# A four-layer graph network on one core: the check of the adjacency lists, with a count on VectorE replaced by a sum on ScalarE

## The chip, the cores and the metric

The kernel runs on one core of a Trainium2 chip. The metric is the device time of one execution in microseconds (us). The engines are named as in the profile: PE is TensorE (PEld its weight loads), DVE is VectorE, ACT is ScalarE, POOL is GpSimd, SP is SyncE, which here issues most DMAs. A `q` behind an engine's name (SPq, ACTq) is its sequencer, which issues DMAs and waits on semaphores.

## The reference, cut to what matters

The input `x` has 16 batches of 1024 nodes by 256 features, and `adj` is one 1024 x 1024 float32 matrix that all batches share. An entry of `adj` is either zero or lies between 0.05 and 0.19; a row has 16.7 entries on average, 30 at most, and none is negative. Layer 0 is the one that the change belongs to:

```python
pre_u = jnp.einsum('bud,dk->buk', h_t, W1[:d])
pre_v = jnp.einsum('bvd,dk->bvk', h_t, W1[d:])
hidden = jax.nn.relu(pre_u[:, :, None, :] + pre_v[:, None, :, :] + b1)
S = jax.nn.sigmoid(jnp.einsum('buvk,ko->buvo', hidden, W2)[..., 0] + b2[0])
a_t = jnp.einsum('buv,bud->bvd', S * A_a, h_t)          # A_a is adj
m_t = jnp.einsum('uv,bud->bvd', A_m, h_t) * h_t          # A_m is adj
z_t = beta1 * h_t + beta2 * (a_t @ Wa + ba) + beta3 * (m_t @ Wm + bm)
```

Since `S` is multiplied by `adj`, the scores of an edge matter only where `adj` isn't zero. Layer 1 multiplies by `adj` and a weight, with a relu and a residual; layers 2 and 3 are graph attention with a softmax over `leaky_relu(f_i + f_j) + adj`.

## The kernel before, in words

Everything is float32. A stage of preparation comes first; after it a branch (`tc.If(listed > 0)`, L688) chooses between a path by lists, which computes the edge scores only at the non-zero entries, and a dense path that computes all of them. With these inputs the lists are taken.

The preparation (L375 to L516) has two threads that are interleaved in the source.

The first thread is layer 0's projections of the first group of four batches (`first_group`, L381). For each batch, PE transposes `h` (16 transposes, L310), ACT copies the four banks into `hT` (`evacuate`, L143; in this stage `by_scalar` is true, so all four copies are ACT's), and `edge_sides` (L315) multiplies `hT` by `w1`: 64 matmuls (L131) per batch, whose banks ACT copies into `st` (L333, L334), and whose results SP stores to DRAM. `hT` is the stationary operand of these matmuls, so none can begin before its copy is done.

The second thread makes the lists: for each of the eight 128-row tiles of `adj` (`adj_sb[:, t, :]`, loaded by SP at L392 behind the first two batches of `x`), DVE finds the 32 largest entries of each row by four MAX8 (L451) and three MATCH_REPLACE8 (L453). At L447 it also counts the row's non-zero entries, into `there`. Afterwards (L473 to L503) a few small DVE instructions and three small matmuls (L468, L470, L489) work out whether the lists hold everything: the number of positive slots must equal the number of entries, no value may occur twice in a row, none may exceed 16, and the rows with more than 16 entries must fit a table. The result is `ok`, which every engine loads (L518) before the branch.

The generator `work` is stepped by `more(n)` at fixed places in the source, but the order in which the instructions stand on each engine is not the source's: the framework schedules the whole program statically, engine by engine, by estimated ready times. An engine then takes its instructions strictly in that order, each waiting on the semaphores that it names.

After the branch, PE's work is ordered by hand (messages, edges, layer 1, attention), and the edge scores (gathers by POOL, adds by DVE, sums by ACT) are paced beside it by a `Side` object that spends a fixed share of a step per microsecond of PE's estimated work. Many of the loads are tied to matmuls by `paced`.

Of the kernel before, what the change touches and what calls it, by code (L numbers as in the profile page):

```python
# [11 lines left out]
F32 = mybir.dt.float32  # L12
I32 = mybir.dt.int32
U32 = mybir.dt.uint32
AF = mybir.ActivationFunctionType
ALU = mybir.AluOpType
AX = mybir.AxisListType
P = 128
# [6 lines left out]
SLOTS = 32  # L25
# [45 lines left out]
def gnn_stack_kernel(  # L71
# [27 lines left out]
    nc = tc.nc  # L99
    B, N, D = x.shape  # L100
    NT = N // P
# [174 lines left out]
    slot_a = const.tile([P, NT, SLOTS], F32, name="slot_a")  # L276
# [98 lines left out]
    with ExitStack() as stack:  # L375
        prep = stack.enter_context(tc.tile_pool(name="prep", bufs=4))
        prep1 = stack.enter_context(tc.tile_pool(name="prep1", bufs=1))
# [54 lines left out]
        def clear():  # L432

            if zeros:
                paced(nc.scalar.dma_start(zeros.pop(0), zero))

        def more(n):
            for _ in range(n):
                next(work, None)


        there = prep1.tile([P, NT], F32, name="there")
        for t in range(NT):
            more(4)
            row = adj_sb[:, t, :]
            left = prep.tile([P, N], F32, tag="left", name="left")
            nc.vector.tensor_scalar(left, row, 0.0, 0.0, ALU.not_equal, ALU.add, accum_out=there[:, t : t + 1])  # L447
            src = row
            for r in range(SLOTS // 8):
                s = slice(8 * r, 8 * r + 8)  # L450
                nc.vector.max(out=slot_a[:, t, s], in_=src)  # L451
                if r < SLOTS // 8 - 1:
                    nc.vector.match_replace(  # L453
                        out=left, in_to_replace=slot_a[:, t, s], in_values=src, imm_value=-1.0
                    )
                    src = left
            if t > 2:
                clear()
                clear()
# [13 lines left out]
        held = prep1.tile([P, NT, SLOTS], F32, name="held")  # L473
        nc.vector.tensor_scalar(held, slot_a, 0.0, None, ALU.is_gt)
        counts = prep1.tile([P, 4], F32, name="counts")
        nc.vector.tensor_reduce(counts[:, 0:1], held, AX.XY, ALU.add)
        nc.vector.tensor_reduce(counts[:, 1:2], there, AX.X, ALU.add)
        nc.vector.tensor_reduce(counts[:, 2:3], slot_a[:, :, 0], AX.X, ALU.max)
        twice = prep1.tile([P, NT, SLOTS - 1], F32, name="twice")
        nc.vector.tensor_tensor(twice, slot_a[:, :, 1:], slot_a[:, :, : SLOTS - 1], ALU.is_equal)  # L480
        nc.vector.tensor_tensor(twice, twice, held[:, :, 1:], ALU.mult)
        nc.vector.tensor_reduce(counts[:, 3:4], twice, AX.XY, ALU.add)
        missed = prep1.tile([P, 1], F32, name="missed")
        nc.vector.tensor_tensor(missed, counts[:, 0:1], counts[:, 1:2], ALU.not_equal)
        nc.vector.tensor_tensor(missed, missed, counts[:, 3:4], ALU.add)
        nc.vector.scalar_tensor_tensor(missed, counts[:, 2:3], TOP, missed, ALU.is_gt, ALU.add)
        more(1)
# [951 lines left out]
    with arm.Else():  # L1439
        with ExitStack() as stack:  # L1440
            wide = stack.enter_context(tc.tile_pool(name="dwide", bufs=9))
            row = stack.enter_context(tc.tile_pool(name="drow", bufs=6))
# [124 lines left out]
```

## Time and profile before

| what | value |
|---|---|
| median of 3 runs | 3131.87 us (3128.81 to 3140.97) |
| the profiled execution, its own time | 3123.77 us |
| its span in the trace | 3122.0 us |
| granted TensorE clock in it | 0.998 |
| busy: PE, PEld, DVE, ACT, POOL | 3071.5, 2181.0, 2422.3, 1821.7, 1894.7 us |
| preparation: last matmul of the first group ends, branch taken | about 101.6 us from the span's start |

The profile's times are those of one execution. A row of the timeline gives the start and the duration in us, the engine, the source line, the operation, the tiles written and read, how many instructions the row merges, and in brackets how long the engine had been idle before it and what released it. A row of the windows gives for one stretch the busy time of each engine, the granted clock, and the busy share and the rate of the DMA engines.

### The profile page before, as it was taken

The page shows a single profiled execution, that of the slowest core. Times are in us where ns is not written, and L with a number is a line of the kernel's source. Part 1 is how long each engine was busy: PE and PEld are TensorE (multiplying, and loading weights), DVE is VectorE, ACT ScalarE, POOL GpSimd, SP SyncE. Part 2 cuts the span into 40 slices and gives each one's busy share as a digit, 9 for nine tenths or more (in the row PEclk, how much of TensorE's full clock was granted, in tenths as well). Part 3 has the DMA queues.
Part 4 walks back from the last instruction along what each step waited for, and adds up shares of the span by engine and source line. Part 5 has one row for each costly group of instructions (what it writes and reads, how often), then busy time and mean ns, then how long its engine had stood idle before and what let it go on. Part 6 is the DMA issues. An engine that isn't in the chain of part 4 may idle for free. (4 is left out here: it accounts for less than half of the span.)

```text
span 3122.0 us, 39040 instructions
## 1 busy us (share of the span) xinstructions
PE 3071.5 (98%) x11954; PEld 2181.0 (70%) x11954; DVE 2422.3 (78%) x3247; ACT 1821.7 (58%) x6456; POOL 1894.7 (61%) x1483
## 2 busy tenths in 40 slices
PE   8999999999999999999999999999999999999999
PEld 5544545545547756888875688887568888858888
DVE  7887777778776878999887899988789983257844
ACT  3345555566655766777667677766667762214242
POOL 1156778777665777667677776676777751076600
PEclk9999999999999999999999999999999999999999
DMA  9998888888889777558977655897765554475500
GB/s 322 330 339 302 278 296 266 272 248 254 263 268 347 233 224 209 155 163 279 304 234 214 201 160 166 271 301 236 215 196 157 165 205 158 137 254 158 162 1 28
DMA packets 288420, 699.96 MB, mean 224 GB/s; under 512 B 46141, under 2 KB 141178, under 8 KB 281034
## 3 DMA queue, kind: packets, MB, share of 16 engines
q0 software_dynamic: 128224, 387.80, 42.0%
q1 hardware_dynamic: 132538, 258.46, 23.5%
q10 hardware_dynamic: 27440, 51.13, 4.4%
q8 instruction: 96, 1.57, 0.2%
q14 instruction: 122, 1.00, 0.1%
HBM read 565.83 MB, written 131.41 MB: 223 GB/s over the span
## 5 line engine op out<-in xcount | busy, mean ns | idle before, releaser
L831 ACT ACTIVATE z<-z 128x256 f32<-128x256 f32 x2432 | 979.7, 406 | 585.6 <-DVE z L827 523.0
L825 DVE TENSOR_TENSOR z<-z,u 128x1024 f32<-128x1024 f32 x608 | 738.3, 1219 | 299.1 <-PE bank L131 174.4
L131 PE MATMUL bank<-feats,m 128*128 128x257 f32 x4096 | 908.7, 380 | 1.1 <-ACT feats L1016 0.7
L708 POOL DMA_INDIRECT z<-v_d,slot_v x512 | 665.4, 1300 | 367.1 <-ACT z L831 196.8
L131 PEld LDWEIGHTS bank<-feats,m 128*128 128x128 f32 x4096 | 769.5, 190 | 111.1 <-ACT feats L1016 1.5
L713 POOL DMA_INDIRECT dense_d<-gt,slot_at x512 | 682.5, 1333 | 196.4 <-issue 139.3
L827 DVE SCALAR_TENSOR_TENSOR z<-z,w2r 128x1024 f32<-128x1024 f32 x608 | 737.3, 1219 | 9.3
L131 PE MATMUL bank<-gc,hw 128*128 128x256 f32 x2048 | 451.1, 382 | 14.9 <-ACT gc L1133 10.2
L831 ACT ACTIVATION_READ_ACCUMULATOR z<-z 128x1 f32 x2432 | 461.6, 190 | 0.0
L131 PE MATMUL bank<-adj_sb,h 128*128 128x512 f32 x1024 | 443.0, 592 | 4.4 <-ACT st L333 2.1
L131 PEld LDWEIGHTS bank<-gc,hw 128*128 128x128 f32 x2048 | 388.8, 191 | 76.8 <-ACT gc L1133 13.3
L1099 DVE SCALAR_TENSOR_TENSOR m<-rho,tau,adj_sb 128x512 f32<-128x512 f32 x512 | 375.7, 742 | 66.0 <-PE bank L131 61.7
L131 PE MATMUL bank<-adjT_in,y 128*128 128x512 f32 (+1 forms) x960 | 402.0, 579 | 5.3 <-DMA adjT_in<-adjT_d 3.6
L131 PEld LDWEIGHTS bank<-adj_sb,h 128*128 128x128 f32 x1024 | 194.1, 190 | 244.8 <-issue 239.0
L131 PEld LDWEIGHTS bank<-adjT_in,y 128*128 128x128 f32 x960 | 181.5, 190 | 219.4 <-issue 206.4
L131 PE MATMUL bank<-w,hT 128*128 128x512 f32 (+1 forms) x1024 | 334.0, 486 | 0.0
L131 PEld LDWEIGHTS bank<-w,hT 128*128 128x128 f32 x1024 | 194.5, 190 | 140.9 <-issue 121.9
L1133 ACT ACTIVATE gc<-gd 128x1024 f32<-128x1024 f32 x64 | 133.2, 2082 | 169.9 <-PE bank L131 104.2
L131 PE MATMUL bank<-g_wT,z 128*128 128x257 f32 x1024 | 230.1, 380 | 0.0
L131 PEld LDWEIGHTS bank<-g_wT,z 128*128 128x128 f32 x1024 | 192.2, 190 | 30.0 <-issue 2.9
L708 POOL DMA_INDIRECT z<-v_d,x_node x96 | 125.0, 1303 | 116.8 <-ACT z L831 61.0
L1131 DVE COPY gc<-gd 128x1024 f32<-128x1024 f32 x64 | 71.8, 1122 | 105.8 <-PE bank L131 79.3
(169 smaller groups left out, 2439.1 us busy)
## 6 DMA issues: line engine op xcount, KB each, us to landing
gd<-dense_d SPq DMA_DIRECT2D x128, 512.0 KB
dense_d<-zero ACTq DMA_DIRECT2D x64, 512.0 KB
adjT_in<-adjT_d SPq DMA_DIRECT2D x112, 256.0 KB
h<-in_x_dram SPq DMA_DIRECT2D x19, 1024.0 KB
u_d<-st SPq DMA_DIRECT2D x64, 256.0 KB
v_d<-st SPq DMA_DIRECT2D x64, 256.0 KB
hw_d<-st SPq DMA_DIRECT2D x64, 256.0 KB
u<-u_d POOLq DMA_DIRECT2D x32, 512.0 KB
```

What stands on the lines that cost most here:

```text
L131: recent.append(nc.tensor.matmul(*args, **kw))
L708: return nc.gpsimd.indirect_dma_start(out=dst, out_offset=None, in_=src[:], in_offset=bass.IndirectOffsetOnAxis(ap=at, axis=0), **how,)
L713: return nc.gpsimd.indirect_dma_start(out=dst[:], out_offset=bass.IndirectOffsetOnAxis(ap=at, axis=0), in_=src, in_offset=None,)
L825: paced(nc.vector.tensor_tensor(z, z, u, ALU.add))
L827: nc.vector.scalar_tensor_tensor(zk, zk, 0.0, w2r[:, None, :].to_broadcast([P, GB, D]), ALU.max, ALU.mult)
L831: nc.scalar.activation(zk[:, c, :], zk[:, c, :], AF.Copy, accum_out=s[:, k, c : c + 1])
L1099: nc.vector.scalar_tensor_tensor(m, r[:, cols], ta[:, kt : kt + 1], ea[:, kt, cols], ALU.max, ALU.mult)
L1131: paced(nc.vector.tensor_copy(gc, by_batch), 16)
L1133: paced(nc.scalar.activation(gc, by_batch, AF.Copy), 16)
```

## The change

The count of non-zero entries on DVE (L447) goes. In its place ACT computes relu(-adj) of each tile of rows and accumulates it along the row into `below_zero`; the elements themselves go to a scratch tile `gone` that nothing reads. The test behind it is another one: instead of comparing two counts, it asks whether any row's 32nd largest entry, or any row's sum of negative parts, is above zero. (A row of exactly 32 entries passes the old test and fails the new one; the densest row of these inputs has 30.)

```diff
-        there = prep1.tile([P, NT], F32, name="there")
+        below_zero = prep1.tile([P, NT], F32, name="below_zero")
+        gone = prep1.tile([P, N], F32, name="gone")
         for t in range(NT):
             more(4)
             row = adj_sb[:, t, :]
             left = prep.tile([P, N], F32, tag="left", name="left")
-            nc.vector.tensor_scalar(left, row, 0.0, 0.0, ALU.not_equal, ALU.add, accum_out=there[:, t : t + 1])
+            nc.scalar.activation(gone, row, AF.Relu, scale=-1.0, accum_out=below_zero[:, t : t + 1])
...
-        nc.vector.tensor_reduce(counts[:, 0:1], held, AX.XY, ALU.add)
-        nc.vector.tensor_reduce(counts[:, 1:2], there, AX.X, ALU.add)
+        nc.vector.tensor_reduce(counts[:, 0:1], slot_a[:, :, SLOTS - 1], AX.X, ALU.max)
+        nc.vector.tensor_reduce(counts[:, 1:2], below_zero, AX.X, ALU.max)
...
-        nc.vector.tensor_tensor(missed, counts[:, 0:1], counts[:, 1:2], ALU.not_equal)
+        nc.vector.tensor_tensor(missed, counts[:, 0:1], counts[:, 1:2], ALU.max)
+        nc.vector.tensor_scalar(missed, missed, 0.0, None, ALU.is_gt)
```

In the built program the eight new activations stand first on ACT, ahead of the copies of the first batch's `hT`. The start of ACT's order, before and after (`x8`: eight in a row):

```text
before                                   after
L160 DMA w1 (three issues)               L160 DMA w1 (three issues)
table load                               table load
L143 hT<-bank x4                         L447 gone,below_zero<-adj_sb x8
L333 st<-bank, L334 st<-bank, ...        L143 hT<-bank x4
                                         L333 st<-bank, L334 st<-bank, ...
```

Each of the eight waits for the load of its own tile of rows, and from the second on also for the one before it, since all write `gone`. The orders on PE, POOL and SP are unchanged, and DVE's is the old one without L447, but for a few of the small instructions of the test. One wait of SP moves: the load of the second batch's `h` behind the branch (L290) now waits for the preparation's last use of memory that its `hT` (L299) waited for before.

## The prediction

> **What bounds the kernel now.** I read the page first, for the bound of the whole. Then I took the timelines of PE, ACT and DVE over the first 102 us, where the change lies, and the windows of the stretch in which `adj` arrives.
>
> ```profile
> PE 3071.5 (98%) x11954; PEld 2181.0 (70%) x11954; DVE 2422.3 (78%) x3247; ACT 1821.7 (58%) x6456; POOL 1894.7 (61%) x1483
> ```
>
> PE is busy for 98% of the span, so a stage is worth what it does to PE. The PE timeline of the preparation:
>
> ```profile
> 10.91 1.54 PE L310 MATMUL bank<-ident,h 128*128 128x128 f32 x6 [1.69 <-DMA h<-in_x_dram]
> 12.24 21.50 PE L131 MATMUL bank<-w,hT 128*128 128x512 f32 x64
> 33.58 1.91 PE L310 MATMUL bank<-ident,h 128*128 128x128 f32 x16
> 35.33 20.81 PE L131 MATMUL bank<-w,hT 128*128 128x512 f32 x64
> ...
> 98.75 2.83 PE L131 MATMUL bank<-w,hT 128*128 128x512 f32 x8
> 102.06 7.21 PE L228 MATMUL bank<-ident,adj_sb 128*128 128x128 f32 x64 [0.47 <-ACT st L334]
> ```
>
> The products of batch 0 start at 12.24, and from there PE runs without a gap until 101.6: four batches of 64 matmuls and 16 transposes, then the first work behind the branch at 102.06. PE sets the length of the preparation. The products wait for copies by ACT, whose timeline has two of batch 0's at the top and those of batch 1, four in a row, below:
>
> ```profile
> 7.96 0.60 ACT L143 ACTIVATE hT<-bank 128x512 f32<-128x512 f32 x1 [4.29 <-PE bank L310]
> 8.82 0.60 ACT L143 ACTIVATE hT<-bank 128x512 f32<-128x512 f32 x1 [0.26 <-PE bank L310]
> ...
> 34.22 2.06 ACT L143 ACTIVATE hT<-bank 128x512 f32<-128x512 f32 x4
> ```
>
> So the first two copies, all that the first products need, are done by 9.4. DVE, which makes the lists beside this:
>
> ```profile
> 18.63 1.22 DVE L447 TENSOR_SCALAR_CACHE_REDUCE left<-adj_sb 128x1024 f32<-128x1024 f32 x1 [8.53 <-DMA adj_sb<-in_adj_dram]
> 21.00 1.22 DVE L447 TENSOR_SCALAR_CACHE_REDUCE left<-adj_sb 128x1024 f32<-128x1024 f32 x1
> ...
> 96.15 0.19 DVE L491 COPY total<-bank 128x32 f32<-128x32 f32 x1 [0.98 <-PE bank L470]
> ```
>
> DVE can't begin before the first tile of `adj` lands at 18.63, is then busy without a break until 95.2, and waits 0.98 us for PE's L470 before the last part of the test. It is nearly as long as PE's thread, but it is PE that comes last. The windows say when the rest of `adj` can be there (the last number is the DMA rate in GB/s):
>
> ```profile
> 18.00:20.00 2.00, 2.00 (x7) 1.02 (x6) 1.37 (x3) 0.42 (x2) 0.75 (x2) 1.00 0.92 323
> 20.00:22.00 2.00, 2.00 (x8) 1.18 (x8) 2.00 (x2) 0.98 (x2) 0.00 (x0) 1.00 1.01 364
> 22.00:24.00 2.00, 2.00 (x8) 1.30 (x7) 2.00 (x5) 0.98 (x2) 0.00 (x0) 1.00 1.01 367
> 24.00:26.00 2.00, 2.00 (x8) 1.30 (x7) 2.00 (x4) 0.60 (x1) 0.00 (x0) 1.00 1.02 404
> 26.00:28.00 2.00, 2.00 (x8) 0.99 (x7) 2.00 (x4) 0.62 (x2) 0.00 (x0) 1.00 1.06 375
> 28.00:30.00 2.00, 2.00 (x7) 1.13 (x6) 2.00 (x3) 0.74 (x2) 0.00 (x0) 1.00 1.09 349
> ```
>
> Behind the first tile, seven of 512 KB are to come, 3.67 MB. Filled at these rates from 18.63 on, they are in at 28.6 if nothing else is moved. If the 1 MB of batch 2's `x`, which SP issues at 18.63, comes in between, it is 2.9 us more, 31.5. The trace's record of semaphore updates has the last of the sixteen updates of the last tile at 29.2, and I take that.
>
> **What the change adds: a wait at the head of ACT.** In the built order the eight activations stand ahead of batch 0's four copies. ACT takes its instructions in order, so the copies now wait for the last tile of `adj`, though they need nothing of it. Step by step:
> 1. The last tile lands at 29.2. The tiles come 1.51 us apart on average ((29.2 - 18.63) / 7).
> 2. One activation with its sum costs 1.045 + 0.187 = 1.23 us, by these two rows (ns, least, median, most), the first of the same shape, the second of the read of the accumulator. That is less than 1.51, so the earlier seven are done when the last tile comes, and the eighth ends at 30.45.
>
> ```profile
> L870 ACT ACTIVATE u<-b1r x56: 1039/1045/1084, 102.4 to 2422.0; 128x1024 f32<-128x1024 f32 x56
> L831 ACT ACTIVATION_READ_ACCUMULATOR z<-z x2432: 183/187/252, 148.0 to 2560.5; 128x1 f32 x188
> ```
>
> 3. Two copies from banks that have long been full: 0.60 for one and 2.06 for four gives 0.49 per further one, so 1.09, and 31.55.
> 4. PE loads `hT` as weights, 0.19, and multiplies from 31.75 on, where it was 12.24: **19.5 us later**. With the bounds of the landing it is 18.9 to 21.8.
>
> Queued behind ACT's wait are PE's products of all four batches, the stores of `hT`, `st` and the zeros, the three small matmuls of the test (between the last products), and so `ok` and the branch, for which every engine waits. PE has no gap from 12.24 to 101.6 in which to catch up, so all of that comes 19.5 us later. The loads of `adj` and of batches 2 and 3 stand ahead of these stores on SP's queue and don't move.
>
> The restart itself: the windows show a granted clock of 1.00 throughout, the idle start included, and batch 0's products took 21.50 against 20.81 for batch 1's, so at most 0.69 us is paid for the start today. Today's start also comes out of idle time (1.69 us just before, and more ahead of it), so I add nothing for the new one. A rule speaks against that: the Trainium skill, "TensorE: Matmul & The Clock Gate", section "What's actually happening", has an array that was idle for some 3.4 us at half clock until it has been busy for about as long. By it a restart after 19 us of idleness loses 1.7 us, an estimate from that page, and the shift would be 20.5.
>
> **What it removes from DVE.** Eight L447, 1.15 us each from start to start (18.63 to 19.78), are 9.2 us. In the test a sum over 256 columns of 0.41 becomes one over 8 (0.15 by its neighbour L477), and one instruction of 0.15 is added: 0.1 less together. DVE's thread then ends at 85.9 instead of 95.2. But its next instruction waits for L470, which moves from 95.73 to 115.2, so the time saved becomes idle time, and I credit nothing. If PE weren't the bound of the preparation, up to 9.3 us would be gained.
>
> The moved wait of SP (batch 1's `h`) is for the preparation's last products, done before SP gets there; `gone` is 4 KB per partition, and the orders show nothing else that it displaces. Both at nothing; should the wait decide once, it is in the upper end.
>
> **The sum.** The profiled execution's own time, 3123.77, becomes 3143.3. The median of the runs is 8.1 above it, and I carry the shift over: 3131.87 + 19.5 = **3151.4 us**, 0.62% more. About 0.5%, 15.7 us, is what a measurement of this kernel can tell from no change.
>
> **The rivals.**
> *Given back behind the branch (not slower).* From 102 to 150 PE is busy for only 41.5 of 48 us and the DMA engines are full (share 1.02); it is the one place where PE waits for transfers. If the later start let these drain ahead, PE could win back at most the 6.5 us that it idles there: 13.0 left, 3144.9, within 0.5%. It decides from 3.8 us won back. Against it: everything that fills the DMA engines there is issued behind the branch or paced by matmuls, and the rate is 0 GB/s from 100 to 102, so there is no backlog that more time could drain. 12 in 100.
>
> *The activations don't keep up.* ACT also has a row of 128x1024 at 2.08 us (L1133, strided). At 2.08 + 0.19 the eight need 18.2 us from 18.63, and end at 36.8 instead of 30.45: 6.3 more, 25.8 in all, 3157.7. Against it: `adj_sb` and `gone` are read and written in a row, as L870's are. 6 in 100.
>
> *The gain on DVE counts and the wait doesn't.* If ACT had all of `adj` before its first copy, at about 8 us, and DVE were the bound, 9.3 us fewer: 3122.6, within 0.5%. The first tile lands at 18.63, so the row itself speaks against it. 2 in 100.
>
> *The change doesn't do what it says.* A row of 32 entries would fail the new test and send the kernel down the dense path: 16 x 1024 x 2 relus of 128x1024 at about 1.1 us on two engines are 18 ms. The densest row has 30. Under 1 in 100.
>
> **How the numbers follow.** The forecast has 79 in 100. Of that some 3 fall under 15.7 by the scatter of the runs (12 us between three of before). Some of the larger rivals are over 0.5% as well, so slower gets 0.81; the first and third rival and those 3 give 0.17 for no change; 0.02 is left for faster by something that I don't see. The range runs from 3143 (the first rival, 3144.9, less 2 of scatter) to 3161 (the second, 3157.7, with 3 of scatter); the bounds of the landing, 3150.8 to 3153.7, lie inside.
>
> **What would show it.** In the changed profile ACT should have eight activations of `gone` (L448 in the changed file) between about 18.7 and 30.5, at 1.05 and 0.19 us, before its first L143; PE's first products should start near 31.7, the transposes being done at 12.4; DVE should wait near 29 us for PE's second small matmul; the first transposes of `adj` should start near 121.6 (102.06 + 19.5); and any later landmark, such as the first sum of layer 1 or the end, should be late by the same. It would be wrong if PE's products start before 25, if the delay shrinks between 120 and 170, or if the activations end long after the last tile.

## The result, and the profile after

The changed kernel takes 3161.77 us (median of 7 runs, 3150.25 to 3164.08), the kernel before beside it 3139.5 (7 runs, 3128.81 to 3147.49). The ratio is **1.0067, 95% interval [1.0051, 1.0083]**: slower by 16 to 26 us, where 19.5 were forecast. The time itself lies 10.4 us over the forecast of 3151.4. Of that, 7.6 are the kernel before, which ran at 3139.5 here and not at the 3131.87 that the forecast started from; the difference between the two kernels, which the forecast is about, is 22.3 between the medians. In the second set of experiments below the ratio was 1.0055 [1.0041, 1.0070].

PE's timeline of the changed kernel, cut as that of before (start, duration, what, idle time before it and its releaser):

```profile
10.73 1.54 PE L310 MATMUL bank<-ident,h 128*128 128x128 f32 x6 [1.27 <-DMA h<-in_x_dram]
30.38 22.93 PE L131 MATMUL bank<-w,hT 128*128 128x512 f32 x64 [18.11 <-ACT hT L143]
53.15 1.91 PE L310 MATMUL bank<-ident,h 128*128 128x128 f32 x16
54.90 20.81 PE L131 MATMUL bank<-w,hT 128*128 128x512 f32 x64
...
118.32 2.83 PE L131 MATMUL bank<-w,hT 128*128 128x512 f32 x8
121.62 7.20 PE L228 MATMUL bank<-ident,adj_sb 128*128 128x128 f32 x64 [0.47 <-ACT st L334]
```

The transposes are done at 12.3 as before. Then PE stands still for 18.11 us, for a copy by ACT. From batch 1 on the rows are those of before, 19.57 us later (54.90 against 35.33), and so are the first transposes behind the branch, 19.56 (121.62 against 102.06). What ACT does meanwhile, the first and the last of the eight activations:

```profile
18.75 1.06 ACT L448 ACTIVATE gone<-adj_sb 128x1024 f32<-128x1024 f32 x1 [15.08 <-DMA adj_sb<-in_adj_dram]
19.72 0.19 ACT L448 ACTIVATION_READ_ACCUMULATOR gone<-adj_sb 128x1 f32 x1
...
28.70 1.06 ACT L448 ACTIVATE gone<-adj_sb 128x1024 f32<-128x1024 f32 x1
29.66 0.19 ACT L448 ACTIVATION_READ_ACCUMULATOR gone<-adj_sb 128x1 f32 x1
29.75 2.04 ACT L143 ACTIVATE hT<-bank 128x512 f32<-128x512 f32 x4
```

ACT idles 15.08 us for the first tile of `adj`, while the banks that it could copy fill up, all four by 12.3. The copies start at 29.75. And DVE, which was to be relieved:

```profile
85.92 0.16 DVE L488 SCALAR_TENSOR_TENSOR missed<-counts,missed 128x1 f32<-128x1 f32 x1
115.72 0.19 DVE L493 COPY total<-bank 128x32 f32<-128x32 f32 x1 [29.65 <-PE bank L471]
```

It is through with its lists at 86.1 instead of 95.2, and waits 29.65 us for PE instead of 0.98.

This one profiled execution has a span of 3162.4 us, 40.4 more than the one of before, and only half of that stands at the branch. The sums of edge scores on ACT, matched one by one between the two traces, are 19.4 us late at 148 us, 25.4 at 723, 31.0 at 908, 28.8 at 1124 and 39.4 at the end. I take what is added behind the branch for scatter of this execution and not for a part of the change: the medians differ by 22.3 us, and the profile of the same kernel in the second set (e6_after) has a span of 3146.6, 24.6 more than that of before. The last section says what the scatter goes with.

### The profile page after: what moved, and what is told of

It reads as the page before. It is cut to its first block, busy times and chain, and to the rows that moved or that the text cites. A ratio compares the mean times of both kernels' runs of the same rounds, so it can differ in the third digit from the quotient of the medians.

```text
span 3162.4 us, 39048 instructions
## 1 busy us (share of the span) xinstructions
PE 3083.4 (98%) x11954; PEld 2186.0 (69%) x11954; DVE 2414.5 (76%) x3232; ACT 1831.1 (58%) x6472; POOL 1905.9 (60%) x1483
## 3 DMA queue, kind: packets, MB, share of 16 engines
q8 instruction: 96, 1.57, 0.2%
## 5 line engine op out<-in xcount | busy, mean ns | idle before, releaser
L710 POOL DMA_INDIRECT z<-v_d,slot_v x512 | 653.7, 1277 | 370.6 <-ACT z L833 202.2
L131 PEld LDWEIGHTS bank<-gc,hw 128*128 128x128 f32 x2048 | 390.1, 192 | 83.0 <-ACT gc L1135 12.3
```

The lines of the kernel that those rows point to most:

```text
L131: recent.append(nc.tensor.matmul(*args, **kw))
L710: return nc.gpsimd.indirect_dma_start(out=dst, out_offset=None, in_=src[:], in_offset=bass.IndirectOffsetOnAxis(ap=at, axis=0), **how,)
```

## The experiments

My theory: the loss is a wait, for the last tile of `adj`, at the head of ACT's queue; it delays PE's first products, and the delay is carried unchanged to the end. The rivals: the work of the eight activations, the scratch tile or the new test costs it wherever they stand; the saving on DVE is a gain that the wait hides; the idle start brings on a slower clock later. The first four kernels ran on one chip, the last two on another, each set with the kernel before beside it.

**e1_late: the same work, without the wait at the head.**

```diff
-            nc.scalar.activation(gone, row, AF.Relu, scale=-1.0, accum_out=below_zero[:, t : t + 1])
+            paced(nc.scalar.activation(gone, row, AF.Relu, scale=-1.0, accum_out=below_zero[:, t : t + 1]))
```

`paced` adds a wait for a recent product. In the built order the first activation then stands behind the copies of batch 0's `hT`, and the other seven are spread over the four batches.

> The changed kernel with its eight activations tied to matmuls of the first group, so that in the built order they stand between the copies of the four batches and no longer ahead of batch 0's. Nothing else differs; the same work is done. Theory (the loss is the wait at the head of ScalarE's queue): PE's first products start near 12.2 us again, the first transposes of adj near 102, and the time is that of the kernel before within 0.2%. Rival (the eight activations, the new test or the scratch tile cost this wherever they stand): still 0.5 to 0.8% slower, about 20 us.

Measured: 3134.82 us (12 runs) against 3128.13 (29), ratio 1.0021 [1.0005, 1.0037]. PE's first products and the first transposes of `adj`:

```profile
12.55 22.14 PE L131 MATMUL bank<-w,hT 128*128 128x512 f32 x64
...
103.15 7.21 PE L228 MATMUL bank<-ident,adj_sb 128*128 128x128 f32 x64 [0.47 <-ACT st L334]
```

The 20 us at the branch are gone but for 1.1 (0.3 in the start, 0.6 in batch 0's products). The time, though, lay 4.8 us over before by the means and 6.7 by the medians, with an interval clear of zero, which the theory hadn't in it. The mean granted clock of its runs was lower, 0.9960 against 0.9967. So the kernel was run again.

**e5_late_again: the same kernel once more.**

> The kernel of e1_late once more, to settle whether its 0.21% [0.05, 0.37] over before is real. Theory (only the wait costs; the branch was 1.1 us late in e1_late, from the phase of the slow clock at the start): 0 to 0.1%, with an interval that holds zero or nearly so. Rival (the eight activations, the scratch tile or the new test cost some 5 us behind the branch wherever they stand): again 0.15 to 0.25%, and the changed kernel beside it would owe the same 5 us to them, so that its branch comes 16 and not 19.6 us late.

Measured: 3132.17 us (12 runs) against 3132.16 (17), ratio 1.0003 [0.9991, 1.0015].

```profile
11.75 22.35 PE L131 MATMUL bank<-w,hT 128*128 128x512 f32 x64
...
102.56 7.21 PE L228 MATMUL bank<-ident,adj_sb 128*128 128x128 f32 x64 [0.47 <-ACT st L334]
```

The surplus of e1_late did not come back, and this time the clocks were alike (0.9967 against 0.9965). When they don't stand in front of PE's first copies, the eight activations, the scratch tile and the new test cost little: the two sets together, weighted by their intervals, give some 0.1% and at most 0.2% (an estimate: 3 us, at most 6), and not 20 us. Whether it is nothing or 3 us stays open.

**e2_wait: the wait, without the work.** The kernel before, with two lines more:

```diff
         there = prep1.tile([P, NT], F32, name="there")
+        seen = prep1.tile([P, 1], F32, name="seen")
+        nc.scalar.activation(seen, adj_sb[:, NT - 1, 0:1], AF.Copy)
```

> The kernel before, count on VectorE and old test included, with one 128x1 copy of an element of the last tile of adj put first on ScalarE: the wait alone, with some 0.2 us of work. Theory: ScalarE is held until the last tile lands at 28.7 us; with 0.2 for the copy and 0.6 for the first eviction PE starts near 29.6 instead of 12.2, batch 0's products take 22.9 instead of 21.5 as in the changed kernel, and everything behind is 18 to 19 us late: 0.5 to 0.7% slower. Rival (the work, not the wait): no more than 0.2 us, so the same as before.

Measured: 3149.88 us (6 runs) against 3128.13, ratio 1.0065 [1.0042, 1.0088]. ACT's timeline and PE's:

```profile
28.82 0.20 ACT L444 ACTIVATE seen<-adj_sb 128x1 f32<-128x1 f32 x1 [25.14 <-DMA adj_sb<-in_adj_dram]
28.93 2.04 ACT L143 ACTIVATE hT<-bank 128x512 f32<-128x512 f32 x4
```

```profile
29.56 23.97 PE L131 MATMUL bank<-w,hT 128*128 128x512 f32 x64 [16.91 <-ACT hT L143]
...
121.84 7.21 PE L228 MATMUL bank<-ident,adj_sb 128*128 128x128 f32 x64 [0.47 <-ACT st L334]
```

One instruction of 0.20 us costs as much as the whole change: 21.75 between the medians against 22.3. PE starts at 29.56, where 29.6 was expected, and the branch is 19.78 us late. This is the plainest evidence for the theory and against the work.

**e3_one: the activation for the first tile alone.** The sums of the other seven tiles are left out.

```diff
-            nc.scalar.activation(gone, row, AF.Relu, scale=-1.0, accum_out=below_zero[:, t : t + 1])
+            if t < 1:
+                nc.scalar.activation(gone, row, AF.Relu, scale=-1.0, accum_out=below_zero[:, t : t + 1])
...
-        nc.vector.tensor_reduce(counts[:, 1:2], below_zero, AX.X, ALU.max)
+        nc.vector.tensor_reduce(counts[:, 1:2], below_zero[:, 0:1], AX.X, ALU.max)
```

> The changed kernel with the activation for the first tile of adj alone; the sums of the other seven tiles are left out, and the test looks at the one sum. Theory (what counts is which tile is waited for): the first tile lands at 18.7 us, 1.25 for the activation and 0.6 for the first copy give PE's first products near 20.6, 8.4 later than before, and with a slow restart of up to 1.4 the branch is 8.4 to 9.8 late: 0.25 to 0.35% slower. Rival (the work): an eighth of 20, 2.5 us.

Measured: 3138.63 us (12 runs) against 3128.13, ratio 1.0029 [1.0014, 1.0045], which is 4.4 to 14 us.

```profile
20.73 22.45 PE L131 MATMUL bank<-w,hT 128*128 128x512 f32 x64 [8.06 <-ACT hT L143]
...
111.49 7.21 PE L228 MATMUL bank<-ident,adj_sb 128*128 128x128 f32 x64 [0.47 <-ACT st L334]
```

With the first tile to wait for, the branch is 9.43 us late, and the time 9.1 us more by the ratio (0.0029 x 3128.13). The rival's 2.5 lies outside the interval. What is waited for sets the cost. Of the work, only the last activation stands in the path, between the landing and the copies: the copies of the changed kernel start 1.05 us behind the start of its eighth activation (28.70 to 29.75).

**e4_no_count: the saving on DVE alone.** The kernel before, with the count and the comparison left out and nothing put in their place but the test of the 32nd largest:

```diff
-            nc.vector.tensor_scalar(left, row, 0.0, 0.0, ALU.not_equal, ALU.add, accum_out=there[:, t : t + 1])
...
-        nc.vector.tensor_reduce(counts[:, 0:1], held, AX.XY, ALU.add)
-        nc.vector.tensor_reduce(counts[:, 1:2], there, AX.X, ALU.add)
+        nc.vector.tensor_reduce(counts[:, 0:1], slot_a[:, :, SLOTS - 1], AX.X, ALU.max)
...
-        nc.vector.tensor_tensor(missed, counts[:, 0:1], counts[:, 1:2], ALU.not_equal)
+        nc.vector.tensor_scalar(missed, counts[:, 0:1], 0.0, None, ALU.is_gt)
```

> The kernel before without the count and with nothing in its place: the sum on VectorE and the comparison with it are left out, and the test asks only whether a 32nd largest entry is above zero. Theory (VectorE's 9.2 us are off the path, since its next instruction waits for a matmul between PE's last products): VectorE waits some 10 us instead of 1 for that matmul, the first transposes of adj start at 102 as before, and the time is the same within 0.2%. Rival (the saving on VectorE is a gain that the wait hid in the changed kernel): 9 us faster, 0.3%.

Measured: 3132.46 us (12 runs) against 3128.13, ratio 1.0005 [0.9990, 1.0020]. DVE's timeline, and PE's behind it:

```profile
96.31 0.19 DVE L488 COPY total<-bank 128x32 f32<-128x32 f32 x1 [10.34 <-PE bank L468]
```

```profile
102.22 7.21 PE L228 MATMUL bank<-ident,adj_sb 128*128 128x128 f32 x64 [0.47 <-ACT st L334]
```

The 9.2 us have turned into idle time (10.34 instead of 0.98), the branch stands where it stood, and a gain of 9 us (0.3%) is outside the interval. There was nothing for the change to win on DVE.

**e6_after: the changed kernel on the chip of e5_late_again.**

> The changed kernel itself, on the same chip as e5_late_again. Theory: the first transposes of adj 19 to 21 us later than 102, the median 19 to 22 us over before, and 17 to 21 us over e5_late_again. Rival (half of the 40 us between the two profiles is a slower clock that the idle start brings on later in the run): the mean granted clock of its runs is lower than before's by 0.002 or more, and the difference nearer 30 us.

Measured: 3149.81 us (6 runs) against 3132.16 (17), 17.65 more; ratio 1.0055 [1.0041, 1.0070]; 17.64 over e5_late_again.

```profile
30.49 23.21 PE L131 MATMUL bank<-w,hT 128*128 128x512 f32 x64 [18.27 <-ACT hT L143]
...
122.01 7.21 PE L228 MATMUL bank<-ident,adj_sb 128*128 128x128 f32 x64 [0.47 <-ACT st L334]
```

The branch is 19.95 us late; the difference of the medians is 1.4 us under the expected range, and the interval (12.8 to 21.9 us) holds 19.95. The mean granted clock of its six runs is 0.9963, that of the 17 of before 0.9965, and e2_wait, which has the same idle start, had 0.9968 against 0.9967. So the idle start doesn't bring on a slower clock later, and that rival falls. (The seven runs of the changed kernel in the result had 0.9954; for the kernel before beside them the clocks aren't on record, so that set can't say.)

No version came out that beats both kernels; the best of the changed ones, e5_late_again, equals the kernel before within its interval.

## Why the prediction was right, point by point

*The path.* Right. The landmarks that show it stood where the prediction had them, or near: the activations between 18.75 and 29.85 (18.7 and 30.5), the first transposes of `adj` at 121.62 (121.6), DVE's wait 29.65 (29). Two did not. PE's first products came at 30.38 and not near 31.7, for the reasons below, and the end of the profiled execution was 40.4 us late and not 19.5. Of the wait, the runs show that it alone is enough (e2_wait) and that without it little or nothing is lost (e5_late_again).

*The terms of the sum.* The total at the branch was right to 0.1 us, partly by luck, since three terms were off and cancelled.
- The landing of the last tile was taken as 29.2, from the record of semaphore updates in the profile of before. By the same record it was 28.61 in the changed kernel and 28.80 in e2_wait, so it moves by some tenths of a us from run to run. The windows alone had given 28.6.
- Step 3 counted two copies before the first product. PE's products begin behind the first: the copies start at 29.75, PE at 30.38. Each product takes one half of the features, and the first of a pair needs only the first copy, 0.49 us less. With copies that start 0.70 earlier (29.75 against 30.45), and a weight load of 0.19 that the start of PE's row turned out to include (the rows of the first product and of its weight load both start at 30.38), this put PE's start 1.37 us too late (31.75 against 30.38).
- "I add nothing" for the restart was wrong, by 1.43 us: batch 0's products took 22.93 us, not 21.50.

*The clock of the restart.* The reason for that last miss is worth a look. PE's weight loads of these products (start, duration):

```profile
33.11 0.34 PEld L131 LDWEIGHTS bank<-w,hT 128*128 128x128 f32 x1 [0.52 <-DVE slot_a L452]
...
35.52 0.19 PEld L131 LDWEIGHTS bank<-w,hT 128*128 128x128 f32 x1 [0.24 <-issue]
```

and the windows of the same stretch, whose granted clock is the third number from the end:

```profile
30.00:34.00 4.00, 3.62 (x5) 1.55 (x6) 4.00 (x6) 1.79 (x4) 0.00 (x0) 1.00 1.00 355
```

The first loads take 0.34 instead of 0.19, and from start to start they are 0.85 us apart (33.11 to 33.96) instead of 0.43 (35.52 to 35.95). So the array runs at half speed there, while the window says 1.00. The trace's list of clock records explains it: the first one, at full clock, begins at 34.50 (13.63 in the profile of before), and where there is no record the window shows 1.00. I had read that default as a measurement. With the start of the first record, the cost of the restart follows in all eight profiles: it is half the time from PE's first product to that record (all in us).

| profile | first product | first full-clock record | half the time between | batch 0's products less 20.81 |
|---|---|---|---|---|
| before | 12.24 | 13.63 | 0.70 | 0.69 |
| e4_no_count | 11.84 | 14.37 | 1.26 | 1.25 |
| e1_late | 12.55 | 15.24 | 1.35 | 1.33 |
| e5_late_again | 11.75 | 14.86 | 1.56 | 1.54 |
| e3_one | 20.73 | 23.86 | 1.57 | 1.64 |
| after | 30.38 | 34.50 | 2.06 | 2.12 |
| e6_after | 30.49 | 35.17 | 2.34 | 2.40 |
| e2_wait | 29.56 | 35.76 | 3.10 | 3.16 |

So the four kernels that start near 12 us pay between 0.69 and 1.54, and the profile of before happens to be the lowest of them: part of the 1.43, and up to 0.9 us of every comparison with its 102.06, is luck of that one execution. The slow stretches differ because the clock is changed on a grid of time that doesn't begin with the products: in each profile all clock records start a whole number of 3.413 us apart (80 records, to within 0.01 us). In the changed kernel the full clock came at 34.50, with the end of the first window of the grid, 31.08 to 34.50, that PE filled; in e2_wait PE filled 82% of a first window, and had to go through a second at half speed. (In the profile of before a window filled to 80% was enough, so how full is full enough stays open.)

The rule that the prediction set against its own row, the Trainium skill's "TensorE: Matmul & The Clock Gate", section "What's actually happening", was the better guide: an idle array falls to half clock. The estimate of 1.7 us for the restart that was worked out from that page, 1.0 more than the 0.69 paid before, compares with 2.12 measured, 1.43 more. The same section says that the window runs freely, with about 3.4 us as its figure; the grid of 3.413 us agrees, and by it the slow stretch ends with the first window that PE fills; in the four kernels that start late it ended 3.1 to 6.2 us after the first product.

*Carried to the end.* Right, as far as these runs can tell. Lateness at the branch (one execution) and loss of time (from the ratio), in us: e4_no_count 0.2 and 1.6, e5_late_again 0.5 and 0.9, e1_late 1.1 and 6.6, e3_one 9.43 and 9.1, e2_wait 19.78 and 20.3, the changed kernel 19.56 and 21, e6_after 19.95 and 17.2. Within the intervals it is one to one, but for e1_late, whose interval starts at 1.6.

*The rivals.* Given back behind the branch: only a little. By the last of PE's waits in that stretch (147.94 in the profile of before) the delay had shrunk from 19.56 to 18.74 us in the changed kernel, from 19.95 to 18.37 in e6_after and from 9.43 to 6.67 in e3_one, and had grown from 19.78 to 20.25 in e2_wait. That is at most 2.8 of the 6.5 us, and under the 3.8 that would have decided; the interval of the changed kernel, which starts at 16, excludes all 6.5 (13.0 left), though that of e6_after (12.8) doesn't by itself. The prediction also misread that stretch: of those 6.5 us PE waits 5.3 for products by DVE (`mT`, L353) and 1.1 for a copy by ACT, not for transfers, while it does wait 3.6 us for loads later in the run (`adjT_in`). Activations that don't keep up: they took 1.06 and 0.19 us, 1.28 from start to start in the last three, and the eighth started 0.09 us behind the landing of its tile (28.61 to 28.70). DVE's saving as a gain: excluded by e4_no_count. The dense path: not taken.

## What to carry to other kernels

When work moves to an engine with idle time, look at where it stands in that engine's order, and at what it waits for, before counting its duration: here an instruction of 0.2 us that needed a late transfer cost 20 us, because unrelated copies for the busiest engine stood behind it. The static scheduler put it ahead of copies whose operands were ready by 12.3 us, 16 us before its own, so the built order has to be read after the change, and a dependency on work in the right place (here `paced`) puts it back. And a saving on an engine that ends by waiting for another one only makes that wait longer: here DVE's was 0.98 us before, 10.34 with the saving alone, and nothing was gained.

## What the runs showed of the hardware that I had not expected

The array falls to half speed for short stretches in the middle of a run that keeps it 98% busy. The clock records list stretches of 3.41 or 6.83 us at 0.5: between 100 and 3100 us there are three in the profile of before (10.2 us together), seven in that of after (30.7 us), one in e3_one (3.4 us). The products show them: in the profile of after, a record of 0.5 covers 167.6 to 171.0, and six products that start at 166.68 took 4.54 us, where the same six took 2.84 before, half of 3.41 more.

No experiment tried what starts such a stretch, but the eight traces together say what goes ahead of it. In 31 of the 32 stretches, PE's rows fill at most 42% of the window of 3.413 us that ends where the stretch begins (55% in the other one). Of the 7124 windows behind which the full clock went on, none is filled less than 43%. So what goes with such a stretch isn't PE's share over the run but a single window that short waits leave more than half empty, and whether a wait does that depends on where the grid cuts it. Behind the same two waits for DVE's `mT`, for instance, the window was filled to 27% in the profile of after (the stretch at 167.6), and to 54% at the least in that of before (no stretch).

The stretches go with the scatter of the times. Over the 46 runs of the kernel before in the two sets, the mean is 3126.1 us where the mean granted clock was 0.998 or 0.999 (4 runs), 3127.9 at 0.997 (25 runs), 3134.1 at 0.996 (13 runs) and 3136.6 at 0.995 or 0.994 (4 runs). Half speed itself can explain only a part: a stretch costs at most half its length, so the 20.5 us more of them in the profile of after account for some 10 of the 20.8 us that it lost behind the branch, and e4_no_count, with 30.7 us of stretches as well, has a span only 11.8 us over that of before. What the rest is stays open. The two single profiles of the changed kernel differ by 15.8 us (3162.4 and 3146.6), so a difference of this size has to be read at a landmark close behind the change, or from many runs.
